# One more group of hidden tiles through seven products, and weight sums and modulations placed over more pairs

## The chip, the cores and the metric

The kernel runs on one core of one Trainium2 chip. The metric is device microseconds of one execution; lower is better. A core has TensorE (PE, matrix products into PSUM), VectorE (DVE), ScalarE (ACT), GpSimd (POOL, used here to start DMAs that add while they copy) and SyncE (SP, used here to start all other DMAs). Everything is in float32 apart from two small helpers in bfloat16.

## The reference

The reference is one conditioned transformer block on x of 4 x 1024 x 512 (4 batches, 1024 tokens, 512 features), with a condition of 4 x 128, 16 heads of 32 and a hidden width of 2048; the block's result is added to x once more.

```python
def norm(x, t, gw, gb, bw, bb):
    g = (t @ gw.T + gb)[:, None, :]
    b = (t @ bw.T + bb)[:, None, :]
    return g * x * rsqrt(mean(x * x, -1) + 1e-6) + b

def attention(x, Wq, Wk, Wv, Wo):
    q, k, v = (heads(x @ W.T) for W in (Wq, Wk, Wv))
    return merge(softmax(q @ k.T / sqrt(32)) @ v) @ Wo.T

def block(x, t, ...):
    x = x + attention(norm(x, t, g1w, g1b, b1w, b1b), Wq, Wk, Wv, Wo)
    z = norm(x, t, g2w, g2b, b2w, b2b)
    return x + (silu(z @ gate_w.T) * (z @ hid_w.T)) @ out_w.T

result = x + block(x, cond_256, ...)
```

## The kernel before, in words

**Blocks, rounds, pairs.** Tokens are cut into 8 blocks of 512 (`NBLK`), features into 4 tiles of 128 (`C`), the hidden width into 16 tiles of 128 (`NF`). Attention is a loop of 256 rounds (`NR`), numbered g; round r works on 4 heads, 256 queries and 256 keys. A round's scores are copied out of PSUM by ACT into a tile `raw` (`keep`), five rounds later DVE adds the shift and ACT takes the exponential, six rounds later PE multiplies with v (`weighted`) and POOL starts a DMA that adds the tile onto the first one of its four (`accumulate`, line 417; 1 MB). When four rounds are summed, DVE folds the sum (`fold_sum`, line 425), PE sums over partitions (`sums`, line 435) and the heads' outputs are divided.

The feed-forward of a block runs beside the attention of the next, from round 60 (`FS`) on. It is cut into 128 pairs p (`NP_`), block p // 16 and hidden tile p % 16, one pair for two rounds. A pair makes the gate and the hidden matrix of its tile by seven products in place of eight (Strassen's scheme in Winograd's form, on halves of features and tokens): `pair_15`, `pair_26`, `pair_7`, `pair_3`, `pair_4`, with the sums between them on ACT (`take_5`, `copy_156`) and DVE (`add_15`, `sub_5`), then `gate_tanh` on ACT, `gate` and `hidden` on DVE, which leave the hidden tile `h[p]`.

**Outputs.** Four hidden tiles are a group (`FG`). The output products of a group are made while the pairs of the next group run. There are two ways. Up to pair 107 `filler` is used: in each pair one of the four output tiles d is contracted straight over the four hidden tiles (`contract`, 512 columns wide, weights `ow`) and DVE adds it to `res` (`take_contract`, line 604). From pair 108 on `last_filler` is used: two output tiles at a time by seven products (`output_steps`), spread over two pairs. These need the sums of output weights, `output_sums` (line 611) loads the eight weights of half a group's row f into a tile `wt` (two DMAs of 256 KB) and `output_sums_add` (line 617) makes the four sums on DVE; and they need the sums of hidden tiles, `hidden_sums` (line 628), eight DVE instructions. The row f of a group is its number modulo 4, so that four rows serve all groups that are left.

**The last block.** The loop of rounds ends at g = 268 (`END`). Pairs 100 to 103 lie in its last eight rounds, where attention drains; block 7's output projection lies in rounds 264 to 267. A second loop, from line 1083, holds pairs 104 (`p0`) to 127 without attention beside them. Block 7's second norm is made there: the root and reciprocal behind pair 104, scale (DVE) and modulation (ACT) of all four feature tiles behind pair 105 (`norm_rest`). Its tokens' sums for the seven products are made around pair 111.

**What sets the order.** PE, DVE, ACT and POOL run their instructions in the order in which the program names them (`manual_schedule`). `pin`, `between` and `after` put a step at the start, behind the middle or at the end of a round. SP is not in that list: each of its DMAs is placed by the planner, which may put it ahead of its place in the program. Tiles with one tag share a fixed number of slots; those of tag `raw` (10 slots) are the attention tiles `raw`, the weights `wt` and the hidden sums `ht`. In the compiled program of before no tile of a tag is handed out ahead of one that the program names before it.

The lines that matter are 611 to 636, 869 to 886, 912 to 1050 and 1083 to 1126.

Of the kernel before, what the change touches and what calls it, by code (L numbers as in the profile page):

```python
# [10 lines left out]
F32 = mybir.dt.float32  # L11
# [6 lines left out]
P = 128  # L18
NB = 512
# [5 lines left out]
def tile_cond_transformer_block(  # L25
# [17 lines left out]
    NF = gh_w.shape[0]  # L43
    QB = NBLK // B
# [4 lines left out]
    FG = 4  # L49
# [9 lines left out]
    ps_av = ctx.enter_context(tc.tile_pool(name="ps_av", bufs=1, space=PSUM))  # L59
    ps = ctx.enter_context(tc.tile_pool(name="ps", bufs=2, space=PSUM))  # L60
# [57 lines left out]
    raw, rmax, shift, mT, av, acc, avs, oT = {}, {}, {}, {}, {}, {}, {}, {}  # L118
    x2, res, h, fw, ow = {}, {}, {}, {}, {}
# [79 lines left out]
    def norm_scale(dst, tag: str, c: int):  # L199
        nc.vector.tensor_tensor(dst[:, c, :], dst[:, c, :], state[tag], ALU.mult)  # L200

    def norm_mod(which: int, b: int, dst, c: int):
        nc.scalar.activation(  # L203
            dst[:, c, :],
            dst[:, c, :],
            AF.Identity,
            bias=mod[:, (2 * which + 1) * C + c, b : b + 1],
            scale=mod[:, 2 * which * C + c, b : b + 1],
        )
# [33 lines left out]
    def norm_rest(which: int, b: int, dst, tag: str):  # L243
        for c in range(C):
            norm_scale(dst, tag, c)
            norm_mod(which, b, dst, c)
# [370 lines left out]
    def output_sums_add(f: int, k: int):  # L617
        w = state["wt", f, k]
        a11, a12, a21, a22, s1, s2, s3, s4 = (w[:, i : i + 2, :] for i in range(0, 16, 2))
        nc.vector.tensor_tensor(s1, a21, a22, ALU.add)  # L620
        nc.vector.tensor_tensor(s2, s1, a11, ALU.subtract)  # L621
        nc.vector.tensor_tensor(s3, a11, a21, ALU.subtract)  # L622
        nc.vector.tensor_tensor(s4, a12, s2, ALU.subtract)  # L623
# [4 lines left out]
    def hidden_sums(gr: int):  # L628
        t = sb.tile([P, 4, 2, HQ], F32, tag="raw", name=f"ht{gr}", bufs=RAW)
        one, two = hidden_halves(gr, 0), hidden_halves(gr, 1)  # L630
        for i in range(4):
            for k in range(2):
                b11, b12, b21, b22 = one[k][:, LEFT], one[k][:, RIGHT], two[k][:, LEFT], two[k][:, RIGHT]
                a, b = ((b12, b11), (b22, t[:, 0, k]), (b22, b12), (b21, t[:, 1, k]))[i]
                nc.vector.tensor_tensor(t[:, i, k], a, b, ALU.subtract)  # L635
        state["ht", gr] = t
# [59 lines left out]
    NR = NBLK * C * (NB // HQ) * UN  # L696
# [17 lines left out]
    def after(g, fn, *a):  # L714
        ended.setdefault(g, []).append((fn, a))
# [21 lines left out]
    for b in range(1, B):  # L737
        for half in range(QB):
            s = math.ceil((len(queue) + 1) / PACE)
            s4 = s - 4 - (s - 6) % UN  # L740
            tag = f"a{b}_{half}"
# [10 lines left out]
    FS = BS + 28  # L752
# [3 lines left out]
    for n in range(NBLK):  # L756
        g0 = (n + 1) * BS
        pin(g0 + 6, load_res, n)
        e = g0 if n == 0 else g0 - 4
        go = e + 13 if n < NBLK - 1 else g0 + 8  # L760
        for d in range(C):
            first.append((go, None, project_out, (n, d)))
            pin(go - 3 + (d // 2 * 4 if n else 0), load_wo, n, d)
        if n < NBLK - 1:
            tag = f"f{n}"
            after(e + 16, add_res, n)
            for k in range(2):
                after(e + 15 + k, lambda n=n, tag=tag, k=k: norm_squares(x2[n], tag, k))
            if n == 0:
                between(e + 17, norm_mean, tag, False)  # L770
            else:
                amid.setdefault(e + 17, []).append((norm_mean, (tag, True)))
            after(e + 17, norm_compact, tag)
            after(e + 19, take, tag)
            after(e + 21, root, tag)
            after(e + 22, invert, tag)
            after(e + 22, put, tag)
            after(e + (23 if n == 0 else 24), norm_spread, tag)
            scales, mods = ((24, 24, 25, 25), (25, 25, 26, 26)) if n == 0 else ((22, 22, 24, 24), (23, 23, 25, 25))
            for c in range(C):  # L780
                after(g0 + scales[c], lambda n=n, tag=tag, c=c: norm_scale(x2[n], tag, c))
                between(g0 + mods[c], lambda n=n, c=c: norm_mod(1, n // QB, x2[n], c))
            for i in range(4):
                after(g0 + (26, 26, 27, 28)[i] - (n > 0 and i == 0), token_sums, n, i)
    for m in range(NBLK * C):
        if m:
            for qh in range(NB // HQ):
                pin(m * MS - 2 + UN * qh, load_queries, m, qh)
            for u in range(UN):
                pin(m * MS - 3 + u, load_keys, m, u)  # L790
        for u in range(UN):
            pin(m * MS + 3 + u, load_v, m, u)
# [19 lines left out]
    with tc.manual_schedule(  # L812
# [51 lines left out]
        g = 0  # L864
        END = NR + 12
        NP_ = NBLK * NF
        seven = ((END - FS) // 2 // FG + 1) * FG

        def filler(p: int, tail: bool = False):

            q = p - FG
            if q < 0:
                evict = chain(-1)
                return (lambda: None), (lambda: None), evict
            if tail:
                pp = ps_av.tile([P, NB], F32, tag="av", name=f"pc{q}")
            else:
                pp = ps.tile([P, NB], F32, tag="w", name=f"pc{q}")
            if q + 1 < seven - FG:
                load_ow(q + 1)  # L880
            half = FG // 2
            return (
                (lambda: contract(q, pp, range(half))),
                (lambda: contract(q, pp, range(half, FG))),
                (lambda: take_contract(q, pp)),
            )
# [10 lines left out]
        while g < END:  # L897
# [10 lines left out]
            p = (g - FS) // 2  # L908
# [45 lines left out]
            if not ffn:  # L954
                if x_on:
                    exponential(r_x)
                evict = chain(g, FG)
# [22 lines left out]
            elif even:  # L980
# [10 lines left out]
                one, two, evict = filler(p)  # L991
# [13 lines left out]
            else:  # L1005
                extra = due or len(queue) > FG
                evict = None
                if kind == 3 and extra:
                    evict = chain(g)
# [9 lines left out]
                if kind == 1:  # L1019
                    gate_tanh(p)  # L1020
                    if extra:
                        spare_bank[0] = True
                        evict = chain(g)
# [24 lines left out]
            if g == FS + 2 * FG - 2:  # L1048
                load_ow(0)
            g += 1  # L1050
        assert not (pinned or amid or halfway or ended or queue or first)
        n = NBLK - 1
        squares = []
# [4 lines left out]
        p0 = (END - FS) // 2  # L1058
# [14 lines left out]
        def last_filler(p: int):  # L1073

            gr, i = (p - FG) // FG, p % FG
            if i % 2 == 0:
                steps[gr, i // 2] = output_steps(gr, i // 2)
            one, five, two_six, seventh, three, four = steps[gr, i // 2]
            if i % 2 == 0:
                return (lambda: (one(), five())), two_six, (lambda: None)  # L1080
            return (lambda: (seventh(), three())), four, (lambda: None)

        for p in range(p0, NP_):
            if p + 2 < NP_:
                load_f(p + 2)
            if p < p0 + NF // FG:
                for k in range(2):
                    output_sums((seven // FG - 1 + p - p0) % (NF // FG), k)
            pair_26(p)
            copy_156(p)  # L1090
            if p == n * NF - 1:
                token_sums(n, 0)
                token_sums(n, 1)
                token_sums(n, 2)
            one, two, evict = filler(p, True) if p < seven else last_filler(p)
            one()
            pair_7(p)
            sub_5(p)
            pair_3(p)
            gate_tanh(p)  # L1100
            gate(p)
            if p + 1 < NP_:
                pair_15(p + 1)
                take_5(p + 1)
                add_15(p + 1)
            pair_4(p)
            hidden(p)
            if p == n * NF - 1:
                token_sums(n, 3)
            two()  # L1110
            evict()
            if p == p0:
                pm = ps.tile([P, NB], F32, tag="w", name=f"pmf{n}")
                for c in range(C):
                    nc.tensor.matmul(pm, ones_mean, squares[c], start=(c == 0), stop=(c == C - 1))
                inv = sb.tile([P, NB], F32, tag="tot", name=f"invf{n}", bufs=1)
                nc.scalar.activation(inv, pm, AF.Sqrt, bias=eps)
                nc.vector.reciprocal(inv, inv)
                state[f"f{n}"] = inv
            if p == p0 + 1:  # L1120
                norm_rest(1, n // QB, x2[n], f"f{n}")
            if p0 + 1 < p <= p0 + 1 + NF // FG:
                for k in range(2):
                    output_sums_add((seven // FG - 1 + p - p0 - 2) % (NF // FG), k)
            if p % FG == FG - 1 and p >= seven - 1:
                hidden_sums(p // FG)
        one, other = (output_steps(NP_ // FG - 1, k) for k in range(2))
        one[0]()
# [45 lines left out]
```

## Time and profile before

| what | value |
|---|---|
| three runs | 2426.95, 2425.57, 2425.66 us; median 2425.66 |
| the profiled execution | 2425.87 us, span 2424.1 us |
| mean granted TensorE clock | 0.998 |
| PE busy | 2374.3 us (98%) |
| DVE busy | 1975.1 us (81%) |
| ACT busy | 1420.1 us (59%) |
| DMA | 499.79 MB, mean 206 GB/s |

In a timeline each line gives the start and the length in microseconds, the engine, the source line and operation, what is written and read, and the number of instructions merged; in brackets stands the idle time of the engine before it and what ended it. SPq lines are DMA issues, not transfers. Line 113 is the helper `mm`, so products are told apart by their tiles: `pa` and `pb` belong to a pair, `pc` to a straight contraction, `outs` to seven output products, `po` to the output projection, `sum` to the softmax sums. Matmul ends are modelled; start to start is the safer measure.

### The profile page before, as it was taken

To read this page: it belongs to the slowest core of one execution; us is meant where nothing else is said; L and a number is where in the kernel's file an instruction comes from. 1 tells how busy PE (TensorE), PEld (TensorE's weight loads), DVE (VectorE), ACT (ScalarE), POOL (GpSimd) and SP (SyncE) were. 2 spreads that over 40 slices of the span, in tenths; PEclk is the share of its full clock that TensorE was granted. 3 is DMA by queue.
4 is the path that set the end of the run, shared out by engine and by line. 5 is a ranking of instruction groups with operands and counts; after the bars stand their busy time and mean duration, and the time that the engine had idled before them with its cause. 6 is when DMAs were issued, how large, how long until landed. Compare 5 with 4: busy or idle time off the path is not lost. (4 is left out here: it accounts for less than half of the span.)

```text
span 2424.1 us, 74021 instructions
## 1 busy us (share of the span) xinstructions
PE 2374.3 (98%) x33149; PEld 1153.2 (48%) x33149; DVE 1975.1 (81%) x2295; ACT 1420.1 (59%) x1519; POOL 172.4 (7%) x207
## 2 busy tenths in 40 slices
PE   9999999999999999999999999999999999989999
PEld 4333434345454544544454545454545454434665
DVE  2688888889799988998899979997999799835544
ACT  4677776766566656665576657665666576412111
POOL 0000000000000000000000000000000000000000
PEclk9999999999999999999999999999999999999999
DMA  6699999889888888889888888898887988862331
GB/s 226 188 295 254 262 251 241 222 220 239 199 203 212 204 226 199 216 212 229 196 211 217 221 201 213 202 238 202 206 210 197 231 197 219 209 213 82 126 106 53
DMA packets 184843, 499.79 MB, mean 206 GB/s; under 512 B 21191, under 2 KB 78535, under 8 KB 157134
## 3 DMA queue, kind: packets, MB, share of 16 engines
q0 software_dynamic: 28656, 208.68, 44.4%
q1 hardware_dynamic: 155582, 286.37, 35.0%
q8 instruction: 261, 4.28, 0.7%
q14 instruction: 56, 0.46, 0.1%
q10 hardware_dynamic: 288, 0.01, 0.0%
HBM read 244.34 MB, written 41.97 MB: 118 GB/s over the span
## 5 line engine op out<-in xcount | busy, mean ns | idle before, releaser
L390 DVE TENSOR_TENSOR raw<-raw,shift 128x2048 f32<-128x2048 f32 (+1 forms) x320 | 588.8, 1857 | 26.1 <-ACT shift L385 26.1
L344 ACT COPY raw<-sc 128x2048 f32<-128x2048 f32 x256 | 479.4, 1873 | 186.2 <-PE sc L337 127.8
L393 ACT ACTIVATE raw<-raw 128x2048 f32<-128x2048 f32 x256 | 490.7, 1917 | 147.5 <-DVE raw L390 145.3
L349 DVE TENSOR_TENSOR rmax<-rmax,raw 128x1024 f32<-128x1024 f32 x384 | 469.5, 1223 | 47.6 <-ACT raw L344 41.0
L113 PE MATMUL pc<-h,ow 128*32 128x512 f32 x3328 | 379.9, 595 | 2.5 <-ACT raw L393 1.5
L417 POOL DMA_DIRECT2D raw<-raw x192 | 165.3, 861 | 1940.7 <-ACT raw L393 839.0
L337 PE MATMUL sc<-q,k 32*128 32x256 f32 x4096 | 293.3, 400 | 0.8 <-ACT raw L344 0.8
L403 PE MATMUL av<-raw,v 128*32 128x256 f32 x4096 | 272.5, 384 | 21.3 <-ACT raw L393 20.8
L113 PE MATMUL pa<-x,fa 128*32 128x256 f32 x4096 | 270.0, 381 | 3.5 <-DVE pa L551 2.5
L113 PE MATMUL pa<-sums,fw 128*32 128x256 f32 x4096 | 267.9, 379 | 0.0
L337 PEld LDWEIGHTS sc<-q,k 32*128 32x128 f32 x4096 | 185.0, 184 | 117.1 <-issue 74.9
L113 PE MATMUL pkq<-y,wkq 128*32 128x512 f32 (+1 forms) x1664 | 230.8, 596 | 0.9 <-ACT y L203 0.7
L113 PEld LDWEIGHTS pc<-h,ow 128*32 128x32 f32 x3328 | 103.7, 110 | 206.9 <-issue 193.0
L113 PEld LDWEIGHTS pa<-x,fa 128*32 128x32 f32 x4096 | 123.3, 110 | 112.1 <-DVE pa L551 20.9
L113 PEld LDWEIGHTS pa<-sums,fw 128*32 128x32 f32 x4096 | 133.1, 110 | 87.9
L403 PEld LDWEIGHTS av<-raw,v 128*32 128x32 f32 x4096 | 110.6, 109 | 134.5 <-ACT raw L393 48.7
L113 PE MATMUL pb<-x,fw 128*32 128x256 f32 x2048 | 134.7, 379 | 1.2 <-ACT pb L566 1.2
L113 PE MATMUL pa<-x,fw 128*32 128x256 f32 x2048 | 134.0, 379 | 0.0
L113 PE MATMUL pb<-sums,fa 128*32 128x256 f32 x2048 | 133.9, 379 | 0.0
L583 ACT ACTIVATE t<-pa 128x512 f32<-128x512 f32 x128 | 78.3, 612 | 92.9 <-PE pa L113 92.6
L113 PEld LDWEIGHTS pkq<-y,wkq 128*32 128x32 f32 (+1 forms) x1664 | 72.6, 117 | 125.3 <-issue 117.4
L385 ACT COPY shift<-sp 128x512 f32<-128x512 f32 x128 | 75.0, 586 | 95.0 <-PE sp L113 95.0
(132 smaller groups left out, 2338.2 us busy)
## 6 DMA issues: line engine op xcount, KB each, us to landing
raw<-raw POOLq DMA_DIRECT2D x192, 1024.0 KB, 9.2
fw<-sw SPq DMA_DIRECT2D x128, 512.0 KB, 7.3
fa<-in_gh_w SPq DMA_DIRECT2D x128, 384.0 KB, 6.1
ow<-in_out_w SPq DMA_DIRECT2D x104, 256.0 KB, 3.6
wkq<-in_kq_w SPq DMA_DIRECT2D x32, 512.0 KB, 5.8
v<-vs SPq DMA_DIRECT2D x128, 128.0 KB, 6.4
k<-kqs SPq DMA_DIRECT2D x124, 128.0 KB, 6.8
kqs<-st SPq DMA_DIRECT2D x61, 256.0 KB, 8.0
```

The lines of the kernel that those rows point to most:

```text
L113: nc.tensor.matmul(dst[k : k + n, :], w[:, k : k + n], moving, start=start, stop=stop, skip_group_check=seeded)
L337: nc.tensor.matmul(sc[:, i, k, :], keys[rows, k * P : (k + 1) * P], queries[rows, :], start=True, stop=True)
L344: nc.scalar.copy(raw[r].rearrange("p k h q -> p h k q"), state.pop(("sc", r)))
L349: nc.vector.tensor_tensor(rmax[j], rmax[j], raw[r][:, k, :, :], ALU.max)
L385: nc.scalar.copy(shift[j][:, k : k + 2, :], pp)
L390: nc.vector.tensor_tensor(t, t, s.unsqueeze(1).to_broadcast(list(t.shape)), ALU.add)
L393: nc.scalar.activation(raw[r], raw[r], AF.Exp)
L403: nc.tensor.matmul(av[j][i * DH : (i + 1) * DH, :], v[m, u][:, k, i * DH : (i + 1) * DH], raw[r][:, k, i, :], start=(kt == 0), stop=(kt == ...
L417: nc.gpsimd.dma_start(out=acc[j].rearrange("p k h q -> p (k h q)"), in_=raw[r].rearrange("p k h q -> p (k h q)"), accum_op=ALU.add,)
L583: nc.scalar.activation(state["t", p], bank_a[p], AF.Tanh, scale=0.5)
```

## The change

Five things are edited.

1. `seven`, the first pair whose filler is made by seven products, goes from 108 to 104. The filler of pairs 104 to 107 is then `last_filler` on group 25 (hidden tiles 100 to 103) in place of four straight contractions; `filler` loses its branch for the tail, and the four loads of `ow` for tiles 100 to 103 go.
2. Group 25 needs row f = 1. Its `output_sums` are put behind rounds 261 and 262 and its `output_sums_add` behind rounds 265 and 266, where before no such step was.
3. `hidden_sums` of group 25 is put between the two loops.
4. The other three rows keep their order 2, 3, 0. Their `output_sums` stand at the start of pairs 105, 106 and 107 (before: 2, 3, 0, 1 at pairs 104 to 107), their `output_sums_add` behind pairs 106, 110 and 114 (before: 106, 107, 108, 109).
5. The scale and modulation of block 7's second norm are made for feature tiles 0 and 1 behind pair 105 and for 2 and 3 behind pair 106 (before: all four behind pair 105).

```diff
+    for k in range(2):
+        after(NR + 5 + k, output_sums, (NR + 12 - FS) // 2 // FG % (NF // FG) - 1, k)
+        after(NR + 9 + k, output_sums_add, (NR + 12 - FS) // 2 // FG % (NF // FG) - 1, k)
...
-        seven = ((END - FS) // 2 // FG + 1) * FG
-
-        def filler(p: int, tail: bool = False):
+        seven = (END - FS) // 2 // FG * FG
+
+        def filler(p: int):
...
-            if tail:
-                pp = ps_av.tile([P, NB], F32, tag="av", name=f"pc{q}")
-            else:
-                pp = ps.tile([P, NB], F32, tag="w", name=f"pc{q}")
+            pp = ps.tile([P, NB], F32, tag="w", name=f"pc{q}")
...
+        hidden_sums(seven // FG - 1)
...
-            if p < p0 + NF // FG:
+            if 0 < p - p0 < NF // FG:
                 for k in range(2):
                     output_sums((seven // FG - 1 + p - p0) % (NF // FG), k)
...
-            one, two, evict = filler(p, True) if p < seven else last_filler(p)
+            one, two, evict = last_filler(p)
...
-            if p == p0 + 1:
-                norm_rest(1, n // QB, x2[n], f"f{n}")
-            if p0 + 1 < p <= p0 + 1 + NF // FG:
-                for k in range(2):
-                    output_sums_add((seven // FG - 1 + p - p0 - 2) % (NF // FG), k)
-            if p % FG == FG - 1 and p >= seven - 1:
+            if p in (p0 + 1, p0 + 2):
+                for c in range((p - p0 - 1) * 2, (p - p0) * 2):
+                    norm_scale(x2[n], f"f{n}", c)
+                    norm_mod(1, n // QB, x2[n], c)
+            for i in range(1, NF // FG):
+                if p == p0 + 4 * i - 2:
+                    for k in range(2):
+                        output_sums_add((seven // FG - 1 + i) % (NF // FG), k)
+            if p % FG == FG - 1:
                 hidden_sums(p // FG)
```

## The prediction

> **What bounds the kernel now.** I read the page first, then PE's timeline from 2050 us on for waits in brackets, then what each wait hangs on, then SP's issues. A difference under 0.2% (4.85 us) is about what a measurement can't tell from none.
>
> ```profile
> PE 2374.3 (98%) x33149; PEld 1153.2 (48%) x33149; DVE 1975.1 (81%) x2295; ACT 1420.1 (59%) x1519; POOL 172.4 (7%) x207
> ```
>
> PE is the bound, so a change pays by PE instructions that go or by PE waits that go. All edits act behind 2086 us. PE's waits of over half a microsecond from 2110 us to the last group are three. The two small ones:
>
> ```profile
> 2206.29 2.93 ACT L203 ACTIVATE x<-x,mod 128x512 f32<-128x512 f32 x4 [3.53 <-DVE x L200]
> 2209.54 1.07 PE L113 MATMUL pb<-x,fw 128*32 128x256 f32 x16 [1.20 <-ACT pb L566]
> ...
> 2228.86 0.75 DVE L635 TENSOR_TENSOR ht<-h 128x256 f32<-128x256 f32 x2
> 2229.33 1.07 PE L113 MATMUL outs<-ht,wt 128*32 128x256 f32 x16 [1.49 <-DVE ht L635]
> ```
>
> The first is pair 106: `copy_156` (L566) stands on ACT behind four modulations. The second is pair 108: `hidden_sums` stands on DVE behind eight adds of weights (2225.93 to 2228.86). The large one is in round 264, pair 102; ahead of it the same step four rounds earlier:
>
> ```profile
> 2120.70 0.61 PE L435 MATMUL sum<-raw,ones_sum 128*32 128x256 f32 x8
> 2121.80 3.64 PE L113 MATMUL pc<-h,ow 128*32 128x512 f32 x32 [0.49 <-ACT total L440]
> 2125.26 1.05 PE L113 MATMUL pb<-x,fw 128*32 128x256 f32 x16
> ...
> 2146.20 1.23 DVE L425 TENSOR_TENSOR raw<-raw 128x1024 f32<-128x1024 f32 x1 [4.98 <-DMA raw<-raw]
> 2147.53 0.90 PE L435 MATMUL sum<-raw,ones_sum 128*32 128x256 f32 x8 [4.98 <-DVE raw L425]
> 2148.89 4.75 PE L113 MATMUL pc<-h,ow 128*32 128x512 f32 x32 [0.47 <-ACT total L440]
> 2153.47 1.04 PE L113 MATMUL pb<-x,fw 128*32 128x256 f32 x16
> ```
>
> PE waits for DVE's fold, the fold for the last accumulating DMA. Behind the wait the contraction takes 4.58 us start to start instead of 3.46, since the granted clock falls to 0.72:
>
> ```profile
> 2147.50:2153.50 6.00, 5.50 (x44) 1.41 (x48) 2.18 (x2) 0.37 (x1) 0.00 (x0) 0.72 0.43 170
> ```
>
> So the wait costs from 2142.37 (end of `pair_26`, 0.87 behind 2141.50) to 2153.47, 11.1 us, where round 260 needs 4.56 from `sum` to `pb`: 6.5 us. Why the DMA is late:
>
> ```profile
> 2112.89 0.86 POOL L417 DMA_DIRECT2D raw<-raw  x1 [10.52 <-ACT raw L393]
> 2123.55 0.86 POOL L417 DMA_DIRECT2D raw<-raw  x1 [9.80 <-DMA raw<-raw]
> 2135.24 0.86 POOL L417 DMA_DIRECT2D raw<-raw  x1 [10.83 <-DMA raw<-raw]
> ```
>
> Three accumulations wait for each other and take 10.7, 11.7 and 10.9 us. The median is 9.2; 2051.03 to 2059.59 shows 8.6. From 2112 to 2146 us the DMA engines are full (share 1.03 from 2124 to 2136). SP shows who shares them:
>
> ```profile
> 2084.32 1.86 ACT L344 COPY raw<-sc 128x2048 f32<-128x2048 f32 x1 [1.86 <-PE sc L337]
> 2086.31 5.00 SPq L614 DMA_DIRECT2D wt<-in_out_w  x3
> ...
> 2113.93 1.21 SPq L614 DMA_DIRECT2D wt<-in_out_w  x2
> ...
> 2129.04 6.56 SPq L614 DMA_DIRECT2D wt<-in_out_w  x6
> ```
>
> The `wt` loads, in the program at pairs 104 to 107 (2182 us on), run 50 to 95 us ahead: the first comes right behind the last `raw` tile (L344), the tile named before it under the same tag.
>
> **The change part by part.**
>
> *Group 25 by seven products.* A product is 16 instructions, 0.8635 us start to start (2136.82, 2137.69, 2138.55). A pair has seven, 6.04 us, and two halves of a straight contraction, 3.45. The new filler has four products in pairs 104 and 106 (3.45, equal) and three in 105 and 107. Two products go: 1.73 us, all on PE's path. Added on ACT per step pair are two copies of 0.37, on DVE 0.42 + 0.42 beside two adds of 0.69 that replace L604's two. The Trainium skill, "TensorE: Matmul & The Clock Gate", section "Back-to-back issue gap", speaks against this: it gives a sustained 81 ns a matmul at 128 columns and 131 at 512, so that halving the columns does not halve the time; about 98 ns at 256 is my estimate between these. By it 112 instructions of 256 cost 1.31 times 64 of 512, and the group would lose 4.3 us instead of winning 1.73. The trace has 54 ns (0.8635 / 16) against 108 (3.45 / 32), exactly half, and the sum stays with it.
>
> *Pair 105, DVE.* The new subtraction and `take` stand behind the reciprocal (end 2200.73) and ahead of `sub_5`: 0.42 + 0.69 + 0.43 put its end at about 2202.2, and `pair_4`, due at 2202.13, waits about 0.1; between 0 and 0.4.
>
> *Modulations in halves.* Two `norm_scale` (0.62 each) and two `norm_mod` (0.73 each) move behind pair 106. ACT is then done with the first two at about 2207.1 and `copy_156(106)` ends near 2207.45, where PE arrives at 2207.4 (0.86 earlier than before). Of 1.20 about 1.1 goes; ends 0.8 and 1.2. Behind pair 106 the copy is ready when PE has 1.4 us of other products to do. Late next would be `sub_5(107)`, behind two scales and eight adds (3.0 us): ended at about 2218.6 for a `pair_4(107)` at 2220.4. Nothing; were the cover gone, 1.2.
>
> *Adds of weights.* Behind pair 107 none is left ahead of `hidden_sums(26)`: it starts 2.8 us earlier, in time for `step_5`. The 1.49 goes; ends 1.2 and 1.49. Behind 110 they meet `token_sums` in pair 111: DVE reaches `sub_5(111)` about 1 us before PE needs it. Behind 114 nothing is near. Four adds behind rounds 265 and 266 (1.5 us each) fit into DVE's idle 3.74 and 3.09 us before 2170.06 and 2174.52. `hidden_sums(25)`, 2.8 us, and one add fit into the idle 3.63 us before 2186.62, and PE needs its first quarter only at 2184.6 (ready 2183.7). Cost nothing; without that cover 3.0 and 2.8.
>
> Sum of the tail: 1.73 + 1.1 + 1.45 - 0.1 = 4.2 us, ends 3.3 and 4.4.
>
> *The loads.* Four `ow` loads (1 MB, issued 2164.90 to 2181.56) go, off every path. Of 16 `wt` loads four (row 1) are now named at rounds 261 and 262 and, as the first behind `raw255`, should still issue at 2086. Then the program names `ht25`, of the same tag, whose writer is DVE behind round 267. If tiles of a tag are handed out in order, the other 12 loads can't be planned before it, and go from 2092-2136 to about 2178 us and later, where the DMA share is 0.2 to 0.4. That the planner keeps to this order the trace shows twice: the first `gh` load (tag shared with ACT's copies) stands at 76.62 us, right behind round 4 where it is named, though `wo`, alone in its tag and named for round 42, was loaded by 31 us; and `wt` started with the last `raw`. From 2112 to 2146 eight `wt` loads go, 2.1 MB; SP's queue moved 6.27 MB there at 48.3% of 34 us, 2.6 us a MB, so 5.5 us of full engines. The accumulations then end at about 2140.6 (bounds: 2146.1 if none moves; 2112.89 + 3 x 8.6 = 2138.7), and DVE is free for the fold at 2141.22. The wait shrinks to 0 to 0.4 us and the clock stays up, as it did behind the 1.49 wait (1.00 from 2229.3 on). Worth: 6.5 at most, 0 at least; I take 6.1, since both bounds but the unmoved one end before DVE is free. What is late next is `pair_26` itself.
>
> The 12 loads pass SP's queue between `fa106` and the loads of pairs 107 and 108. At 0.33 to 1.7 us an issue (1.7 in the full stretch at 2094.93) they take 4 to 20 us. `fw107`, issued at 2187.40, is needed at 2204.7 and lands 7.3 later; about 10 us of delay are covered. Row 2 is needed by DVE behind pair 106 (2214).
>
> Sum: 4.2 + 6.1 = 10.3 us. The profiled execution took 2425.87, span and 1.8 around it, 0.2 above the median; from about 2425.7 this gives 2415.4 us.
>
> **The rivals.**
>
> *The loads stay early.* If the planner may hand `wt` slots out ahead of `ht25`, the DMA stretch is as before and the 4.98 us wait stays: 2425.7 - 4.2 = 2421.5. For it: a free slot is all that a load needs. Against: the order seen above.
>
> *Part relief.* The accumulations have a floor of their own, or `res7` (1 MB at 2127.45) and the weights of pairs fill what is freed; at half the relief the wait is about 2.2, without a clock loss: 6.5 - 2.2 = 4.3, 2417.2. The skill's section "The HAM clock gate" of the same page puts the fall to half clock at an idle window of about 3.4 us; by it any rest below that keeps the 1.1 us of clock too, while the rows only bracket it between 1.49 and 4.98.
>
> *Slower: the late loads come too late.* If SP's order puts row 2 behind the loads of pair 110 (`fw110` 2221.01, `fa110` 2223.6), less 2 us for the tail's gain, plus four issues and 8.5 us to landing it lands at about 2231; `output_sums_add` behind pair 106 blocks DVE and with it `sub_5(107)`, which can stand a landing at 2216. That is 15 us against 10.3: 2430.4. Behind `fa109` (2214.1) it costs 6; the sign turns from `fa110` on. Against: the loads have tiles from about 2183 on and are named ahead of `load_f(108)`.
>
> *Only the arithmetic.* Waits in pairs 106 and 108 come back in other places and the loads stay: 2425.7 - 1.7 = 2424.0.
>
> **How the numbers follow.** Forecast 0.66 (own range 2414.2 to 2417), part relief 0.11, loads early 0.11, arithmetic only 0.04, slower 0.08. The range leaves out 'arithmetic only' and 'slower' and reaches above the early loads: 2421.8. Below, the best ends give 2425.7 - 4.4 - 6.5 = 2414.8; the small waits of the same stretch (0.44, 0.49, 0.15) could go too: 2413.4. Faster by over 0.2% (below 2420.8): forecast and part relief, 0.77. Same: early loads and arithmetic, 0.15. Slower 0.08.
>
> **What would show it.** `wt` loads: four at about 2086, twelve behind 2170; accumulations under 10 us apart; `sum` of round 264 within 0.6 us of `pair_26`; clock 1.00 there; no PE wait over 0.5 us in pairs 106 and 108; `pc` x3200. The forecast is wrong if more than four `wt` loads stand before 2146 us, or if a PE wait behind L620 or a late `fw` shows in pairs 105 to 108.

## The result and the profile after

The changed kernel takes 2416.17 us (median of six runs, 2412.83 to 2421.26) against 2425.61 (2423.93 to 2426.95): a ratio of 0.9965, interval 0.9954 to 0.9976. Repeated beside the experiments it took 2416.72 against 2424.85, ratio 0.9968 (0.9956 to 0.9979). The forecast was 2415.4 in a range of 2413.4 to 2421.8, with faster by over 0.2% as the likeliest side.

The profiled execution of after took 2416.97 us, its span is 2415.2, 8.9 below that of before. Start to start, the 8.9 us lie here:

| stretch | before | after | won |
|---|---|---|---|
| first instruction to `pair_26` of pair 102 | 2140.61 | 2140.93 | -0.32 |
| `pair_26` of pair 102 to its `pair_7` (holds the wait of round 264) | 12.86 | 8.85 | 4.01 |
| on to the start of pair 104 | 28.50 | 28.50 | 0 |
| start of pair 104 to `pair_7` of pair 108 | 48.25 | 43.51 | 4.74 |
| on to the end (the 0.5 lies behind the last group's wait, in the last steps and stores) | 193.9 | 193.4 | 0.5 |

The first and the last row are not the change's: executions of one kernel differ by as much there. The next profile of the changed kernel has 2137.95 and 193.6.

SP's issues in the timeline of after: four `wt` loads stand where sixteen stood, and the other twelve come behind 2174 us, on both sides of a load for the next pairs. The third line is block 7's `res`, 5.4 us earlier than before.

```profile
2086.63 5.70 SPq L614 DMA_DIRECT2D wt<-in_out_w  x3
...
2092.90 0.43 SPq L614 DMA_DIRECT2D wt<-in_out_w  x1
...
2122.05 0.33 SPq L456 DMA_DIRECT2D res<-in_x  x1
...
2174.95 4.34 SPq L614 DMA_DIRECT2D wt<-in_out_w  x7
2183.73 0.33 SPq L531 DMA_DIRECT2D fw<-sw  x1
2184.11 1.75 SPq L614 DMA_DIRECT2D wt<-in_out_w  x2
2186.32 0.33 SPq L529 DMA_DIRECT2D fa<-in_gh_w  x1
2186.70 1.38 SPq L614 DMA_DIRECT2D wt<-in_out_w  x3
```

The accumulations and PE in round 264 of after:

```profile
2113.21 0.86 POOL L417 DMA_DIRECT2D raw<-raw  x1 [9.36 <-ACT raw L393]
2124.01 0.86 POOL L417 DMA_DIRECT2D raw<-raw  x1 [9.95 <-DMA raw<-raw]
2135.49 0.86 POOL L417 DMA_DIRECT2D raw<-raw  x1 [10.62 <-DMA raw<-raw]
...
2141.81 1.05 PE L113 MATMUL pa<-sums,fw 128*32 128x256 f32 x16
2145.21 0.64 PE L435 MATMUL sum<-raw,ones_sum 128*32 128x256 f32 x8 [2.35 <-DVE raw L425]
2146.33 3.64 PE L113 MATMUL pc<-h,ow 128*32 128x512 f32 x32 [0.48 <-ACT total L440]
2149.78 1.05 PE L113 MATMUL pb<-x,fw 128*32 128x256 f32 x16
```

The wait fell from 4.98 to 2.35 us and not to 0.4. The first two accumulations still take 10.8 and 11.5 us; only the last is shorter, 8.4 in place of 10.9. How long each took, and what SP's queue (q1 in the view of the DMA queues) moved beside it:

| accumulation | first | second | third |
|---|---|---|---|
| before | 10.7 us, 1.15 MB | 11.7 us, 2.76 MB | 10.9 us, 2.37 MB |
| after | 10.8 us, 1.20 MB | 11.5 us, 2.34 MB | 8.4 us, 0.49 MB |

The rows of the third (packets, MB, share of 16 engines), before from 2135.2 to 2146.1 us and after from 2135.5 to 2143.8:

```profile
q1 hardware_dynamic: 1155, 2.37, 57.3%
...
q1 hardware_dynamic: 217, 0.49, 17.4%
```

Of the 2.3 MB that went from beside the chain, 1.9 went from beside the third accumulation. The contraction behind the wait has its full speed again (3.45 us start to start), and the stretch's row has a clock of 1.00:

```profile
2145.00:2150.00 5.00, 4.31 (x44) 1.38 (x48) 2.28 (x3) 0.37 (x1) 0.00 (x0) 1.00 0.18 69
```

Pairs 106 and 108 of after, where the two small waits were:

```profile
2203.20 0.36 ACT L566 COPY pb<-pa 128x256 f32<-128x256 f32 x1
2203.66 1.05 PE L113 MATMUL pb<-x,fw 128*32 128x256 f32 x16
...
2219.19 0.75 DVE L635 TENSOR_TENSOR ht<-h 128x256 f32<-128x256 f32 x2
2220.92 1.05 PE L113 MATMUL outs<-ht,wt 128*32 128x256 f32 x16
```

No bracket stands behind either PE line: `copy_156` ends 0.1 us ahead of PE, the first hidden sums about 1 us ahead. From one `pair_7` to the next, pairs 104 to 108 took 13.25, 10.86, 9.50 and 11.18 us before and take 13.26, 8.64, 9.49 and 8.64.

### The profile page after: what moved, and what is told of

It reads as the page before. It is cut to its first block, busy times and chain, and to the rows that moved or that the text cites. A ratio compares the mean times of both kernels' runs of the same rounds, so it can differ in the third digit from the quotient of the medians.

```text
span 2415.2 us, 74223 instructions
## 1 busy us (share of the span) xinstructions
PE 2370.4 (98%) x33245; PEld 1155.5 (48%) x33245; DVE 1978.6 (82%) x2307; ACT 1422.4 (59%) x1523; POOL 172.5 (7%) x207
## 4 chain that ended last, share of the span: by engine, by line
PE 76%; DVE 13%; ACT 5%; DMA 3%; issue 2%; SPq 0%; DVEq 0%; ACTq 0%; POOLq 0%
PE pa L113 18%; PE pc L113 12%; PE sc L337 8%; PE av L403 8%; PE pb L113 8%; PE pkq L113 6%; PE po L113 4%; DVE raw L390 4%; DVE rmax L349 4%; PE outs L113 3%; PE pv L113 3%; PE mt L358 2%; ACT raw L344 2%; PE sp L113 1%; DVE total L443 1%
## 5 line engine op out<-in xcount | busy, mean ns | idle before, releaser
L113 PE MATMUL pc<-h,ow 128*32 128x512 f32 x3200 | 362.8, 594 | 2.5 <-ACT raw L393 1.5
```

What stands on the lines that cost most here:

```text
L113: nc.tensor.matmul(dst[k : k + n, :], w[:, k : k + n], moving, start=start, stop=stop, skip_group_check=seeded)
```

## The experiments

### The changed kernel again

Nothing is edited. It shares the runs of before with the next three.

> The changed kernel once more, beside the next three on the same chip. Six runs of it ranged from 2412.83 to 2421.26 us, wider than the kernel before. Theory: the wait in round 264 is set by when the last accumulating DMA lands and differs from run to run; where it passes a clock window the clock falls as well. Expected 2414 to 2419, ratio about 0.9965, and in the profile a wait of 0 to 3 us in front of `sum` in round 264. Rival: the spread is one of the first runs; then all within 1.5 us of each other.

Measured: 2416.72 us, seven runs from 2411.88 to 2422.49, so the spread is the kernel's own. In this profile the wait in front of `sum` is 1.26 us (2.35 in the other), and the accumulations take 11.0, 9.9 and 8.8 us. Its span is 3.9 us below that of the other profile: 1.1 of it lies in the stretch of pair 102, and 3.0 lie ahead of that, where the first `sum` of the whole kernel already starts 3.1 us earlier (136.90 against 139.98).

```profile
2141.14 0.64 PE L435 MATMUL sum<-raw,ones_sum 128*32 128x256 f32 x8 [1.26 <-DVE raw L425]
```

### Loads early again

```diff
+        for i in range(1, NF // FG):
+            for k in range(2):
+                output_sums((seven // FG - 1 + i) % (NF // FG), k)
         hidden_sums(seven // FG - 1)
...
-            if 0 < p - p0 < NF // FG:
-                for k in range(2):
-                    output_sums((seven // FG - 1 + p - p0) % (NF // FG), k)
```

> The changed kernel with one edit: the loads of rows 2, 3 and 0 are named ahead of `ht25`, so that the planner may place them early again, as in the kernel before. Theory (loads are held by the order of the tag, and holding them shortens the wait): twelve more `wt` loads between 2086 and 2140 us, the wait in front of `sum` of round 264 back to about 5 us (4.98 before) with the clock falling behind it, and a time about 4 us above the changed kernel, 2420 to 2421.5. Rival (the wait shrank for another reason, and the loads don't matter): the wait stays at about 2.4 and the time at 2416 to 2417.

Measured: 2421.22 us (eleven runs, 2419.06 to 2423.23), ratio 0.9985 (0.9976 to 0.9994). SP and PE of this kernel:

```profile
2093.62 7.23 SPq L614 DMA_DIRECT2D wt<-in_out_w  x4
...
2111.45 0.81 SPq L614 DMA_DIRECT2D wt<-in_out_w  x2
...
2126.67 6.71 SPq L614 DMA_DIRECT2D wt<-in_out_w  x6
...
2145.97 1.08 PE L435 MATMUL sum<-raw,ones_sum 128*32 128x256 f32 x8 [4.57 <-DVE raw L425]
2147.53 5.94 PE L113 MATMUL pc<-h,ow 128*32 128x512 f32 x32 [0.48 <-ACT total L440]
```

Naming six tiles ahead of `ht25` instead of behind it brings the loads back to 2093 to 2133 us, the wait back to 4.57 and the slow contraction with it; 4.5 us are lost. The stretch of pair 102 takes 13.83 us, 0.97 more than before, and pair 104 to `pair_7` of pair 108 takes 43.50, as in the changed kernel. What holds the loads is the order within the tag, shown by this one edit.

### Holding the loads, alone

```diff
+        hold = sb.tile([P, 16, P], F32, tag="raw", name="hold", bufs=RAW)
+        nc.vector.memset(hold[:, 0, 0:1], 0.0)
         assert not (pinned or amid or halfway or ended or queue or first)
```

This is on the kernel before.

> The kernel before with one edit: a placeholder tile of tag `raw`, of which DVE sets one element between the two loops, is named ahead of all sixteen `wt` loads. Nothing else of the change is in it: group 25 is contracted straight, adds and modulations stand where they stood. Theory: all `wt` loads issue behind 2170 us, the wait in front of `sum` falls from 4.98 to 2 us or less, the clock stays up, and the time falls by 4 to 6 us to 2419.5 to 2421.5. Rival (the loads don't matter): wait near 5, time 2425.6 within 1 us. A second rival: the sixteen late loads delay pairs 105 to 107, and what is won is given back there; PE waits behind L620 would show it.

Measured: 2419.03 us, ratio 0.9979 (0.9971 to 0.9988), 5.8 us below before and 0.5 below the range expected. In its profile the stretch of pair 102 takes 7.82 us, 5.0 less than before. Its timeline:

```profile
2175.53 3.23 SPq L614 DMA_DIRECT2D wt<-in_out_w  x7
...
2141.91 0.64 PE L435 MATMUL sum<-raw,ones_sum 128*32 128x256 f32 x8 [1.31 <-DVE raw L425]
...
2202.55 1.07 PE L113 MATMUL pb<-x,fw 128*32 128x256 f32 x16 [1.20 <-ACT pb L566]
2222.34 1.07 PE L113 MATMUL outs<-ht,wt 128*32 128x256 f32 x16 [1.48 <-DVE ht L635]
```

A tile that nobody reads wins more than half of what the change wins. From pair 104 to `pair_7` of pair 108 it takes 48.24 us, as before (48.25): the sixteen late loads delay nothing, which rules out the rival that they starve the pairs behind them. With the run above the two halves are apart: loads 5.8 us alone, the rest 3.6 alone (2424.85 - 2421.22), together 8.1. The two sum to 9.4; each has an interval of about 2 us to either side, so this is no sign that they work on each other.

### Modulations whole, adds early, group 25 straight

Three edits of the changed kernel that each undo one part. Each has one run, and the reading is PE's timeline, which agrees to 0.01 us in pairs 104 to 108 between executions of the changed kernel.

```diff
-            if p in (p0 + 1, p0 + 2):
-                for c in range((p - p0 - 1) * 2, (p - p0) * 2):
-                    norm_scale(x2[n], f"f{n}", c)
-                    norm_mod(1, n // QB, x2[n], c)
+            if p == p0 + 1:
+                norm_rest(1, n // QB, x2[n], f"f{n}")
```

> The changed kernel with scale and modulation of all four feature tiles of block 7 behind pair 105, as before. Theory: ACT's four modulations (2.93 us) hold `copy_156(106)` again, PE waits about 1.2 us in front of `pb` of pair 106 and that pair takes about 10.9 us start to start in place of 9.50. Rival (the wait went because PE comes 0.86 us earlier or later): no wait there. From the start of pair 104 to `pb` of pair 108 the changed kernel takes 43.51 us; this one should take 44.9.

```diff
-                if p == p0 + 4 * i - 2:
+                if p == p0 + 1 + i:
```

> The changed kernel with the adds of weights for rows 2, 3 and 0 behind pairs 106, 107 and 108 in place of 106, 110 and 114. Theory: `hidden_sums(26)` stands behind eight adds on DVE again and PE waits about 1.5 us for it in pair 108; from the start of pair 104 to `pb` of pair 108 45.2 us against 43.51. Rival (DVE has room for them now that L604 is gone): no wait and 43.5.

```diff
-            one, two, evict = last_filler(p)
+            one, two, evict = filler(p) if p < p0 + FG else last_filler(p)
```

> The changed kernel with group 25 contracted straight in pairs 104 to 107 (`filler` with its bank of tag `av`, and the four `ow` loads), everything else left: row 1 early, `hidden_sums(25)` made though not used, loads held, modulations in halves, adds spread. This measures the products by themselves. Theory: two products more, 1.73 us, 0.86 in pair 105 and 0.86 in pair 107; from the start of pair 104 to `pb` of pair 108 45.2 us against 43.51. Rival (four more copies and adds of the seven products cost PE waits that eat part of the gain): less than 1.2 us more.

Measured, from the start of pair 104 to `pair_7` of pair 108: 44.90, 45.19 and 45.16 us against 43.51, so 1.39, 1.68 and 1.65 us for the three parts. One line of the first and one of the second:

```profile
2202.72 1.07 PE L113 MATMUL pb<-x,fw 128*32 128x256 f32 x16 [1.19 <-ACT pb L566]
```

```profile
2217.93 1.07 PE L113 MATMUL outs<-ht,wt 128*32 128x256 f32 x16 [1.48 <-DVE ht L635]
```

The old waits come back in their old places and sizes. Straight contraction takes 9.47 us from `pair_7` of 105 to that of 106 and 9.49 from 107 to 108, where the seven products take 8.64 and 8.64. The three add to 4.72, the whole tail won 4.74: the parts are independent.

The straight kernel's profile holds one thing more. Its wait in round 264 was 2.21 us, and yet the contraction behind it was slow:

```profile
2145.75 0.64 PE L435 MATMUL sum<-raw,ones_sum 128*32 128x256 f32 x8 [2.21 <-DVE raw L425]
2146.87 5.34 PE L113 MATMUL pc<-h,ow 128*32 128x512 f32 x32 [0.48 <-ACT total L440]
```

```profile
2146.80:2152.30 5.50, 5.43 (x40) 1.60 (x44) 2.20 (x3) 0.02 (x1) 0.00 (x0) 0.69 0.01 3
```

So in one execution a wait of 2.2 us was followed by the lower clock, where one of 2.35 in another was not.

### A quarter of `res`

```diff
-        nc.sync.dma_start(out=res[n], in_=x[n])
+        nc.sync.dma_start(out=res[n][:, : (1 if n == NBLK - 1 else C), :], in_=x[n][:, : (1 if n == NBLK - 1 else C), :])
...
```

`project_out` of block 7 then reads feature tile 0 for all four.

> The changed kernel with one feature tile of block 7's `res` loaded in place of four (256 KB in place of 1 MB, at about 2122 us) and used for all four; it leaves out adding the other three feature tiles of x. Theory (what is left of the wait is DMA load beside the last three accumulations): 0.75 MB less at 2.6 us a MB is about 2 us, the second and third accumulation take 9 to 9.5 us in place of 11.5 and 9.9 seen in two profiles, and the wait of 2.35 or 1.26 us in front of `sum` goes under 0.4. Rival (a floor of the accumulations themselves): three accumulations of 10 to 11 us still, and the wait stays over 1 us.

Measured, one run: 2413.31 us. The load issued at 2120.00; accumulations and `sum`:

```profile
2111.07 0.86 POOL L417 DMA_DIRECT2D raw<-raw  x1 [9.09 <-ACT raw L393]
2121.64 0.86 POOL L417 DMA_DIRECT2D raw<-raw  x1 [9.71 <-DMA raw<-raw]
2132.13 0.86 POOL L417 DMA_DIRECT2D raw<-raw  x1 [9.63 <-DMA raw<-raw]
...
2141.43 0.64 PE L435 MATMUL sum<-raw,ones_sum 128*32 128x256 f32 x8 [0.71 <-PE pa L113]
```

The second accumulation takes 10.5 us, more than the 9 to 9.5 expected and less than 11.5; the wait is 0.7, in place of 2.35 and not under 0.4. One run against one would say little, since the wait differs between executions. The kernels with modulations whole, adds early and group 25 straight run the same program as after up to round 264, so there are five executions to compare with, and the kernel before with the loads held. The second column is how long the load of `res` issued ahead of `pair_26` of pair 102:

| execution | `res` ahead | second accumulation | wait | stretch of pair 102 |
|---|---|---|---|---|
| after | 18.9 | 11.5 | 2.35 | 8.85 |
| group 25 straight | 18.7 | 11.8 | 2.21 | 10.42 (slow contraction) |
| loads held, kernel before | 19.3 | 11.2 | 1.31 | 7.82 |
| after, again | 24.6 | 9.9 | 1.26 | 7.77 |
| modulations whole | 24.6 | 9.8 | 0.59 | 7.10 |
| adds early | 24.4 | 10.0 | 0.75 | 7.26 |
| a quarter of `res` | 18.8 | 10.5 | 0.71 | 7.23 |

Where the whole `res` issued some 19 us ahead, the second accumulation took 11.2 to 11.8 us; where it issued 24.5 ahead, 9.8 to 10.0; with a quarter 10.5. That `res` is a part of what is left is likely. The wait itself follows it less closely (1.31 in one row, 1.26 in the next), and what moves the load from 19 to 24.5 us ahead between executions is open.

### The last sums on DVE

```diff
+        elif r >= NR - UN:
+            nc.vector.tensor_tensor(acc[j], acc[j], raw[r], ALU.add)
         else:
             nc.gpsimd.dma_start(
```

> The changed kernel, in which the last three accumulations (rounds 253 to 255) are adds on DVE in place of DMAs started by POOL. Theory: the wait that is left in round 264 hangs on that chain of three DMAs; with it gone `sum` follows `pair_26` at once, which is worth the 2.35 us of the profile and on average 2 to 3 us, and the runs should agree better: 2412.5 to 2414.5. Three adds of about 2.3 us each are hidden on DVE, which idles for half of rounds 259 to 262. Rival (DVE takes over as what PE waits for): the adds delay `shifted` or `gate`, PE waits 1 to 2 us more for exponentials between 2106 and 2131, and the time stays at 2416 or above.

Measured: 2414.64 us (five runs, 2412.88 to 2414.84), ratio 0.9955 (0.9943 to 0.9967), 0.1 above the range expected.

```profile
2114.61 2.28 DVE L417 TENSOR_TENSOR raw<-raw,raw 128x2048 f32<-128x2048 f32 x1
...
2121.68 2.28 DVE L417 TENSOR_TENSOR raw<-raw,raw 128x2048 f32<-128x2048 f32 x1
...
2126.93 2.28 DVE L417 TENSOR_TENSOR raw<-raw,raw 128x2048 f32<-128x2048 f32 x1
```

```profile
2140.48 1.05 PE L113 MATMUL pa<-sums,fw 128*32 128x256 f32 x16
2141.48 0.64 PE L437 MATMUL sum<-raw,ones_sum 128*32 128x256 f32 x8
2142.60 3.64 PE L113 MATMUL pc<-h,ow 128*32 128x512 f32 x32 [0.48 <-ACT total L442]
```

Three adds of 2.28 us replace three DMAs of 8.4 to 11.5 us, `sum` follows `pair_26` at once, and the stretch of pair 102 takes 6.46 us, its floor here. PE's waits ahead of it, from 2085 to 2121 us, are those of after, each within 0.02 us. The runs lie within 2 us where those of after lie within 10.6.

### Sums on DVE with early loads, and on the kernel before

The first joins the edits of "Loads early again" and "The last sums on DVE"; the second is the DVE edit alone on the kernel before.

> Both edits together on the changed kernel: the last three accumulations on DVE, and rows 2, 3 and 0 named ahead of `ht25`, so that all `wt` loads run between 2086 and 2140 us again. Theory (early loads cost time through the accumulating DMAs alone): no wait in front of `sum`, time as with the sums on DVE and held loads (2414.64), 2413 to 2415.5. Rival (early loads also hold up something else, such as weights of pairs behind them in SP's queue): 1 to 4 us more, with PE waits for `fa` or `fw`.

> The kernel before with the last three accumulations on DVE and nothing else of the change. Theory: the whole of the wait in round 264 and of the clock behind it goes (12.86 us from `pair_26` to `pb` in the profile of before, 6.46 with the sums on DVE), so 6.4 us: 2418 to 2419.5; waits in pairs 106 and 108 stay at 1.2 and 1.5 us. Rival (without the seven products and the spread adds DVE or the loads make PE wait elsewhere): 2421 or more.

Measured: 2412.42 us (2411.97 to 2413.04), ratio 0.9945 (0.9930 to 0.9960), and 2418.35 us, ratio 0.9969 (0.9956 to 0.9981), beside a before of 2426.35. The first is 0.6 below the range expected. It has its loads early; no bracket stands at `sum` in it, nor in the second, whose line is the last:

```profile
2091.10 9.27 SPq L616 DMA_DIRECT2D wt<-in_out_w  x4
...
2123.72 3.85 SPq L616 DMA_DIRECT2D wt<-in_out_w  x5
...
2140.09 0.64 PE L437 MATMUL sum<-raw,ones_sum 128*32 128x256 f32 x8
...
2144.70 0.64 PE L437 MATMUL sum<-raw,ones_sum 128*32 128x256 f32 x8
```

With the sums on DVE, early loads take 6.47 us in the stretch of pair 102 and 43.51 from pair 104 to 108, against 6.46 and 43.50 with held ones: they cost nothing on PE's path once no accumulating DMA stands on it, so the harm seen here went through that chain. It is the fastest kernel here; it and the one with held loads (2414.64) were measured beside different runs of before, and their intervals overlap, so they are not told apart. In the second kernel the stretch goes from 12.86 to 6.46 us, the 6.4 expected, with both small waits untouched. The medians are 8.0 us apart, with an interval of 4.6 to 10.7; that more than 6.4 is owed to the wait isn't shown.

## Why the prediction was right, point by point

*Where it acts.* Right: PE's time changed at the three waits and in the products of group 25; the stretches between them are equal to 0.01 us.

*Group 25 by seven products*, 1.73 us: measured 1.65, half in pair 105 and half in 107 as worked out. The linear reading of the rows (54 against 108 ns an instruction) holds; by the page's figures that the prediction quotes the group would have lost time, and it did not.

*Modulations in halves*, 1.1: measured 1.39. *Adds of weights*, 1.45: measured 1.68. Both were taken from the brackets, and a bracket counts from the modelled end of the matmul ahead, 1.05 us behind its start, where the next could start after 0.86. So each wait was about 0.19 us longer than its bracket. That is what was mis-sized in the tail.

*Pair 105, DVE*, -0.1: nothing. `pair_4(105)` starts at 2198.48, 0.87 behind the product ahead of it. Sum of the tail 4.2, measured 4.74, above the upper end of 4.4 by what the brackets hide.

*What was costed at nothing* was nothing: `hidden_sums(25)`, the four adds of row 1 and the late adds leave no wait on PE, and the twelve loads passed SP's queue in about 13 us around `fw107`, which issued 3.7 us earlier than before (2183.73 against 2187.40), as pair 104 did.

*The loads*, 6.1: the mechanism is as predicted (loads early again, holding alone), the size was too large: 4.0 us in the profile and 5.1 in the second profile of the same kernel. The step that failed is "the accumulations then end at about 2140.6", got by taking 5.5 us of transfers (2.1 MB at 2.6 us a MB) out of the whole chain. They ended at 2143.9, where DVE's fold starts. About as much went as was reckoned, 2.3 MB, but the chain got only 2.6 us shorter, 1.2 us a MB: nearly all of it went from beside the third accumulation, which took 8.4 us where the prediction's own fastest took 8.6, while the second, 2 us ahead of which `res` now issued, kept 2.34 MB and its 11.5 us. The stretch was not full throughout either, as the prediction reads it: the share from 2112 to 2124 us is 0.83, and the first accumulation took 10.7 us there all the same, and 10.8 after; why is open.

What came, a wait of 2.35 us without a loss of clock, is the rival "part relief" with its 2.2 us, which had a chance of 0.11. Two of the prediction's signs failed with it: accumulations under 10 us apart, and `sum` within 0.6 us of `pair_26`. The others came: four `wt` loads early and twelve behind 2170 us, the clock at 1.00, no wait in pairs 106 and 108, and 3200 instructions of `pc`.

*Total.* 4.74 + 4.01 - 0.32 + 0.5 = 8.9 us of span against 10.3: an underrated tail and an overrated wait partly cancel, and the first and last row add what differs between executions anyway. The medians, 2416.17 and 2416.72, lie between the forecast's 2415.4 and the rival's 2417.2. That the forecast's number is so near is in part luck. The low end of the range, 2413.4, is 0.3 under what its own terms give: 2414.8 less 0.44, 0.49 and 0.15 is 2413.7.

*The rivals.* "The loads stay early" was set at 2421.5; with the loads named ahead of `ht25` the kernel measures 2421.22, but by other terms: a tail that won 4.74 and a stretch of pair 102 that lost 0.97. Its condition was not met. Nor was the slower rival's: row 2's loads stand directly behind `fa106`. "Only the arithmetic" fails on both counts, waits and loads. The page's rule by which "part relief" kept the clock, a fall at an idle window of about 3.4 us, isn't what the straight kernel shows: there it fell behind a wait of 2.21 us and, past `sum`, one of 0.48.

## What to carry to other kernels

A planner that places loads freely is bound by the order in which tiles of one tag are named, so naming one tile moved megabytes of transfers by 50 to 90 us here; look for what those transfers share the engines with before moving any of them. Here the transfer chain that ended on the critical path was better taken off the DMA engines than given a quieter neighbourhood: three adds on an idle VectorE were worth the whole wait, held loads a part of it. Waits read in brackets behind a product are short by the modelled overlap, 0.19 us each here; price them from start to start.

## What the runs showed that was not expected

- Freed DMA time does not come back one to one: with 2.3 MB fewer moved beside it, a chain of three accumulations got 2.6 us shorter (10.7 + 11.7 + 10.9 to 10.8 + 11.5 + 8.4), not 5.5. 1.9 of the 2.3 MB went from beside one of the three.
- The clock's answer to a wait is not set by the wait's length alone: behind 2.21 us it was 0.69 over 5.5 us, behind 2.35 and 1.26 it stayed at full speed, behind 4.98 it was 0.72 over 6 us and behind 4.57 it was 0.56 over 7.1 us (the contraction took 5.94 us instead of 3.64). A fall cost 1.7 us of clock in the first (5.5 x 0.31) and in the third (6 x 0.28), about twice that in the last (7.1 x 0.44 = 3.1). In the first and the third it came with PE already back at work; with the loads early it began ahead of `sum` (0.95 over the 4.9 us before it). What sets the moment wasn't tested.
- The changed kernel scatters over 10.6 us between runs, the same kernel with the last sums on DVE over 2. The wait in round 264 is only a part of it: the two profiles of the changed kernel differ by 3.0 us ahead of round 264 and by 1.1 in the stretch with the wait. The kernel before with the sums on DVE still scattered over 4.4 us: its longest run, 2421.74, is the profiled one, without a wait or a slow contraction, and reaches `pair_26` of pair 102 at 2142.82 us, 2.2 later than the profile of before. No profile was taken of one of the longest runs of the changed kernel, so what makes those long stays open.
